# Graph layer on one core: group 3's gathers one stage later, the next-to-last batch in front of the last pieces, part of the last batch's products ahead of its sums

## The chip, the cores and the metric

The kernel runs on one core of a Trainium2 chip. The metric is the device time of one execution in microseconds. Its engines are TensorE (PE, with its weight loads as PEld), VectorE (DVE), ScalarE (ACT), GpSimd (POOL) and SyncE (SP); each works through its own instructions in program order and waits on semaphores for the others. Sixteen DMA engines move the data. "Group", "batch" and "stage" are explained below. Line numbers such as L618 are those of the kernel before.

## The reference, cut to what matters

One message-passing layer on a graph of 6250 nodes (128 features) and 100000 edges (4 features each), with the edges sorted by destination, and a layer norm on either side of the residual:

```python
msg_in = concatenate([x[src], x[dst], edge_attr], axis=1)
h = silu(msg_in @ mW1 + mb1)
messages = h @ mW2 + mb2
aggregated = segment_sum(messages, dst, num_segments=N)
u = silu(concatenate([x, aggregated], axis=1) @ uW1 + ub1)
updated = u @ uW2 + ub2
y = layer_norm(x + updated, ln_g, ln_b)
out = _layernorm(x + y)
```

All numbers are float32.

## The kernel before

**Set-up stage (L115 to L412).** The product of `msg_in` and `mW1` is split. Two tables are made from x: `tab_a` = x times the rows of `mW1` for the source, `tab_b` = x times the rows for the destination, plus `mb1`. The 49 tiles of 128 nodes are taken in seven parts of eight tiles (`parts`, L354), one part a turn of the loop at L367. In a turn TensorE first turns the next part's tiles around (`turn_x`, L336 to L341; ScalarE copies the result to `xT`), then makes the two tables of this part (L377); ScalarE copies one half (L379), VectorE adds the bias to the other (L380), and SP stores both to DRAM (L383, L384). The last product of each turn is kept in the list `table`. All TensorE results of this stage go through one ring of four PSUM buffers (`wide`).

**Gathers.** The rows of the edges' sources are gathered by GpSimd with indirect DMAs of 128 rows each (`fetch`, L273 to L294, gathers at L277), eight for a group of 1024 edges. There are 98 groups; the last has six tiles. The first five groups (0 to 4, `RAW` = 5) gather rows of x itself, since the table isn't ready, and TensorE multiplies them later (`turn_rows`, L357; L621); the others gather rows of `tab_a`. `fetch(g, *after)` can take two instructions of TensorE: the first of the group's eight gathers then waits for the first of them, the fifth for the second; `None` is no wait. In the set-up stage the gathers are issued at these places: groups 0 and 1 ahead of the loop; `fetch(2, *table)` in turn 1 (waits for the products of turns 0 and 1); `fetch(3, None, table[2])` in turn 2 (the fifth gather waits for the products of turn 2); `fetch(4, *table[3:])` in turn 4 (products of turns 3 and 4); `fetch(RAW, None, turn_rows(2))` after the loop (group 5, which reads `tab_a` and waits for its stores).

**The loop over groups (L675 to L717).** For group g: SP loads rows of `tab_b` and edge attributes for group g+4 (`load`, L580); VectorE adds the gathered rows to TensorE's products (L635) and ScalarE takes the Silu (L636), both in `hidden`; TensorE makes the products of group g+2 (`products`, L618); VectorE makes the 0/1 matrices (`node_matrix` L591, `edge_matrix` L604); TensorE sums the messages by node with 0/1 matrices (`sums`, L647, 16 instructions for eight tiles, after a transpose of the degrees at L642 in every fourth group); VectorE adds the sums to `acc` and, every fourth group, the degrees to `deg` (`add`, L660 and L665). The gathers of group g+2 are issued in turn g; the first waits for the first product of group g+2, the fifth for the first sum of group g (L704).

**Batches of nodes (`node_batch`, L466 to L559).** When all edges of four tiles of nodes have been seen, a batch of these nodes is started, in stages divided by `yield`; the batch is a generator, and `advance` takes each running batch one stage further. The stages are: 1 load of x (L495, after a fill of the unused rows at L494 in the last batch) and, but for the last batch, copies of sums and degrees (L500, L501); 2 the products of x, sums and degrees (L509, L510, L511); 3 the Silu (L514); 4 the bias `ub2` as a product with a row of ones (L516) and the output product (L525); 5 addition of x and moments (L527, L483, L484; L530 adds `b_b` to x); 6 the root (L489); 7 the scaling, the addition of x and the moments of that (the "z stage", L534 to L540, L483, L484); 8 the root of these; 9 their reciprocal and the shift (L547, L549); 10 the output (L555); 11 the store (L559). The loop takes one stage a group, and two from group 92 on (L716). There are twelve batches in the list and a last one of two tiles. The twelfth, of three tiles, called `before` in the code and "the next-to-last batch" here, starts in group 95.

**The end (L719 to L756).** The last group, of six tiles, is done in two pieces of four and two tiles (`piece`, L726 to L729: addition L727, Silu L728, sums L647). The order around them is written out by hand: two more stages of the next-to-last batch, stage 1 of the last batch, the last full group's sums added, piece one, one stage of the next-to-last batch (its z stage), piece two, the last group's sums added, two stages of the last batch, then both batches in turn to their ends. The next-to-last batch has four stages behind it when the loop ends.

Of the kernel before, what the change touches and what calls it, by code (L numbers as in the profile page):

```python
# [18 lines left out]
P = 128  # L19
# [5 lines left out]
def kernel(  # L25
# [247 lines left out]
    def fetch(g, *after):  # L273

        rows[g] = gath.tile([P, G, H], F32, name="ga")
        for i in range(tiles_of(g)):
            ins = nc.gpsimd.indirect_dma_start(  # L277
                out=rows[g][:, i, :],
                out_offset=None,
                in_=x if g < RAW else tab_a[:, :],  # L280
                in_offset=bass.IndirectOffsetOnAxis(
                    ap=src_i[:, g, i : i + 1] if g else src_0[:, i : i + 1], axis=0
                ),
            )
            part, at = divmod(i * len(after), G)
            if after and at == 0 and after[part]:
                tc.add_manual_dep(
                    ins.ins,
                    after[part].ins.name,
                    mybir.DependencyInfo(  # L290
                        mybir.DependencyClass.Sync, mybir.DependencyReason.DATA
                    ),
                    reason="TensorE keeps up with the gathers",
                )  # L294
# [72 lines left out]
    for k, (i0, n) in enumerate(parts):  # L367
        if k + 1 < len(parts):
            turn_x(*parts[k + 1])

        tb = x_sb[:, i0 : i0 + n, :]
        ta = tpool.tile([P, G, H], F32, name="t", bufs=2)
        for j0, m in groups(n, G // 2):
            pm = wide().rearrange("p (i s) f -> p i s f", s=2)
            for j in range(m):
                cols = slice((i0 + j0 + j) * P, (i0 + j0 + j + 1) * P)
                ins = nc.tensor.matmul(pm[:, j], xT[:, cols], w1, start=True, stop=True)  # L377
            own = slice(j0, j0 + m)
            nc.scalar.copy(ta[:, own], pm[:, :m, 0, :])  # L379
            nc.vector.tensor_add(  # L380
                tb[:, own], pm[:, :m, 1, :], b1[:, None, :].to_broadcast([P, m, H])
            )
        nc.sync.dma_start(by_node(tab_a)[:, i0 : i0 + n, :], ta[:, :n])  # L383
        nc.sync.dma_start(by_node(tab_b)[:, i0 : i0 + n, :], tb)  # L384
        table.append(ins)
        if k == 0:
            attributes(0)
        if k == 1:
            fetch(2, *table)
            for t in mv:  # L390
                nc.sync.dma_start(t[W:], mW1[2 * H :])
        if k == 2:
            fetch(3, None, table[2])
        if k == 3:
            destination_lists()
            attribute_rows(0)
            turn_rows(0)
        cols = slice(i0 * P, NW if i0 + n == NT else (i0 + n) * P)
        nc.vector.memset(acc[:, cols], 0.0)
        if k == 4:  # L400
            fetch(4, *table[3:])
            destinations(0)
            load_bases(0)
            turn_rows(1)
# [27 lines left out]
    ub2_row = consts.tile([1, H], F32, name="ub2_row")  # L432
    g_b = consts.tile([P, H], F32, name="g_b")
    b_b = consts.tile([P, H], F32, name="b_b")
    raw_w = {}

    def load_weights():
        for name, shape in (("w2", [P, H]), ("u1a", [P, H]), ("mb2", [P, 1])):
            raw_w[name] = work.tile(shape, F32, name=f"raw_{name}", bufs=1)
        nc.sync.dma_start(raw_w["w2"], mW2)  # L440
        nc.sync.dma_start(raw_w["u1a"], uW1[P:])
        nc.sync.dma_start(raw_w["mb2"], mb2.rearrange("(f o) -> f o", o=1))
        nc.sync.dma_start(u1x, uW1[:P])
        nc.sync.dma_start(u2, uW2)
        nc.sync.dma_start(ub1_col, ub1.rearrange("(f o) -> f o", o=1))
        nc.sync.dma_start(ub2_row, ub2.rearrange("(o f) -> o f", o=1))
        for t, row in ((g_b, ln_g), (b_b, ln_b)):
            nc.sync.dma_start(t, row.rearrange("(o f) -> o f", o=1).to_broadcast([P, H]))

    def fuse_weights():  # L450
# [15 lines left out]
    def node_batch(i0, n, work, new, y, final=False):  # L466

        cols = slice(i0 * P, (i0 + n) * P)
        m = (min((i0 + n) * P, N) - i0 * P) // n
        assert m * n == min((i0 + n) * P, N) - i0 * P  # L470

        def rows_of(t):

            return t[i0 * P : i0 * P + m * n].rearrange("(p j) f -> p j f", j=n)

        def flat(t):
            return t[:, :n].rearrange("p i f -> p (i f)")

        def moments(v):
            mv = work.tile([P, BT, 2], F32, name="mv", bufs=2)  # L480
            for i in range(n):
                st = work.tile([P, 6], F32, name="st", bufs=2)
                nc.vector.bn_stats(st, v[:, i, :])  # L483
                nc.vector.bn_aggr(mv[:, i, :], st)  # L484
            return mv

        def std(mv):
            r = work.tile([P, BT], F32, name="r", bufs=2)
            nc.scalar.activation(r[:, :n], mv[:, :n, 1], AF.Sqrt, bias=eps)  # L489
            return r  # L490

        xs = new("xs")
        if m < P:
            nc.vector.memset(xs[m // 32 * 32 :, :n], 0.0)  # L494
        nc.sync.dma_start(xs[:m, :n], rows_of(x))  # L495
        sums, counts = acc[:, cols], deg[:, cols]
        if not final:

            acc_b, deg_b = new("acc_b"), new("deg_b", DR)
            nc.scalar.copy(flat(acc_b), sums)  # L500
            nc.scalar.copy(flat(deg_b), counts)  # L501
            sums, counts = flat(acc_b), flat(deg_b)
        yield
        xb = xs
        if final:
            xb = new("xb")
            nc.vector.tensor_add(xb[:, :n], xs[:, :n], b_b[:, None, :].to_broadcast([P, n, H]))
        y = y()
        nc.tensor.matmul(flat(y), u1x, xT[:, cols], start=True, stop=False)  # L509
        nc.tensor.matmul(flat(y), w2u, sums, start=False, stop=False)  # L510
        nc.tensor.matmul(flat(y), mb2u, counts, start=False, stop=True)  # L511
        yield
        uT = new("uT")
        nc.scalar.activation(flat(uT), flat(y), AF.Silu, bias=ub1_col)  # L514
        yield
        nc.tensor.matmul(  # L516
            y[:, :n],
            ones[0:1, :],
            ub2_row[:, None, :].to_broadcast([1, n, H]),
            start=True,  # L520
            stop=False,
        )
        by_p = flat(uT).rearrange("k (p j) -> k p j", j=n)
        for i in range(n):
            nc.tensor.matmul(y[:, i, :], by_p[:, :, i], u2, start=False, stop=i == n - 1)  # L525
        yield
        nc.vector.tensor_add(y[:, :n], y[:, :n], xs[:, :n])  # L527
        mv = moments(y)
        if not final:
            nc.vector.tensor_add(xs[:, :n], xs[:, :n], b_b[:, None, :].to_broadcast([P, n, H]))  # L530
        yield
        r = std(mv)
        yield
        nc.vector.reciprocal(r[:, :n], r[:, :n])  # L534
        z = new("z")
        for i in range(n):
            nc.vector.scalar_tensor_tensor(
                y[:, i, :], y[:, i, :], mv[:, i, 0:1], g_b, op0=OP.subtract, op1=OP.mult
            )
            nc.vector.scalar_tensor_tensor(  # L540
                z[:, i, :], y[:, i, :], r[:, i : i + 1], xb[:, i, :], op0=OP.mult, op1=OP.add
            )
        mz = moments(z)
        yield
        rz = std(mz)
        yield
        nc.vector.reciprocal(rz[:, :n], rz[:, :n])  # L547
        shift = work.tile([P, BT], F32, name="shift", bufs=2)
        nc.vector.scalar_tensor_tensor(  # L549
            shift[:, :n], mz[:, :n, 0], -1.0, rz[:, :n], op0=OP.mult, op1=OP.mult  # L550
        )
        yield
        o = z
        for i in range(n):
            nc.scalar.activation(  # L555
                o[:, i, :], z[:, i, :], AF.Identity, bias=shift[:, i : i + 1], scale=rz[:, i : i + 1]
            )
        yield
        (nc.scalar if final else nc.sync).dma_start(rows_of(out), o[:m, :n])  # L559
# [115 lines left out]
    for g in range(NG):  # L675
# [37 lines left out]
        for i0, n, first in batches[:-1]:  # L713
            if g == (first if first >= NG - 3 else first + 1):
                running.append(node_batch(i0, n, *node_tiles(nodes, node_y)))
        for _ in range(2 if g >= NG - 6 else 1):  # L716
            advance(running)  # L717

    g = NG - 1  # L719
# [18 lines left out]
    )  # L738
    while running:
        advance(running)  # L740
    for _ in range(2):
        next(before)
    next(final)

    nc.scalar.activation(primed, ones[0:1, 0:1], AF.Silu)
    add(g - 1, pt.pop(g - 1))
    pt[g] = degrees(g)
    piece(0, n - 2)
    next(before)
    piece(n - 2, n)  # L750
    add(g, pt.pop(g))
    for _ in range(2):
# [161 lines left out]
```

## Time and profile before

| | us |
|---|---|
| median of 3 runs | 1183.07 (1181.99 to 1183.82) |
| the profiled execution | 1183.82 |
| its span, first to last instruction | 1181.7 |
| TensorE busy | 738.3 |
| GpSimd busy | 743.1 |
| VectorE busy | 486.0 |
| ScalarE busy | 239.8 |

The mean clock granted to TensorE is 0.667 of full speed. A line of the timeline has the start and duration in us, the engine, the line of the kernel, the operation, what it writes and reads ("out<-in"), and in brackets the idle time of its engine just before it with what ended it; "remote" is a semaphore whose sender the profile doesn't identify, "issue" is time in which it shows no wait. A line of the groups has the number of instructions, the total and mean duration, and the idle time before them. TensorE's instructions are recorded at their start, and their ends are modelled. A product of float32 shows as two instructions.

### The profile page before, as it was taken

To read this page: it belongs to the slowest core of one execution; us is meant where nothing else is said; L and a number is where in the kernel's file an instruction comes from. 1 tells how busy PE (TensorE), PEld (TensorE's weight loads), DVE (VectorE), ACT (ScalarE), POOL (GpSimd) and SP (SyncE) were. 2 spreads that over 40 slices of the span, in tenths; PEclk is the share of its full clock that TensorE was granted. 3 is DMA by queue.
4 is the path that set the end of the run, shared out by engine and by line. 5 is a ranking of instruction groups with operands and counts; after the bars stand their busy time and mean duration, and the time that the engine had idled before them with its cause. 6 is when DMAs were issued, how large, how long until landed. Compare 5 with 4: busy or idle time off the path is not lost.

```text
span 1181.7 us, 11311 instructions
## 1 busy us (share of the span) xinstructions
PE 738.3 (62%) x3647; PEld 668.7 (57%) x3647; DVE 486.0 (41%) x1016; ACT 239.8 (20%) x297; POOL 743.1 (63%) x790
## 2 busy tenths in 40 slices
PE   5466887655765566557646655756666665656653
PEld 4465775645655565556645654656565565656552
DVE  4361653432523532532443353343343252353344
ACT  2110120320311221220221121121132131122132
POOL 6546666666666566656666665666566666666660
PEclk9787877666566567566666666666666667666665
DMA  8662232232222231223132222232222222222120
GB/s 200 181 167 73 73 82 64 67 82 64 70 67 73 56 81 50 77 65 84 47 83 71 59 57 80 67 81 56 70 74 66 72 72 62 65 56 69 46 59 20
DMA packets 69932, 88.95 MB, mean 75 GB/s; under 512 B 20687, under 2 KB 51550, under 8 KB 69866
## 3 DMA queue, kind: packets, MB, share of 16 engines
q0 software_dynamic: 25024, 51.30, 17.1%
q1 hardware_dynamic: 40264, 34.96, 10.2%
q10 hardware_dynamic: 4578, 1.89, 0.7%
q8 instruction: 31, 0.51, 0.2%
q14 instruction: 35, 0.29, 0.1%
HBM read 76.71 MB, written 11.38 MB: 75 GB/s over the span
## 4 chain that ended last, share of the span: by engine, by line
PE 44%; issue 35%; POOL 12%; DMA 3%; DVE 2%; another core or an unknown queue 2%; SPq 1%; ACT 1%; DVEq 0%; ACTq 0%; POOLq 0%
PE pre L618 20%; PE pt L647 16%; POOL ga L277 12%; PE y L525 2%; PE wide L377 1%; DMA ga<-tab_a,src_i 1%; PE y L516 1%; PE y L509 1%; PE pre L621 1%; PE y L510 1%; PE wide L339 1%; DVE s L635 1%; DMA x_sb<-in_x_dram 1%; PE y L511 1%
## 5 line engine op out<-in xcount | busy, mean ns | idle before, releaser
L277 POOL DMA_INDIRECT ga<-tab_a,src_i x742 | 703.7, 948 | 383.1 <-issue 200.4
L618 PE MATMUL pre<-mv,st 100*128 100x128 f32 x1564 | 343.3, 393 | 227.3 <-issue 197.6
L618 PEld LDWEIGHTS pre<-mv,st 100*128 100x128 f32 x1564 | 314.2, 300 | 244.5 <-issue 219.3
L647 PE MATMUL pt<-oh,h 128*128 128x96 f32 x1564 | 290.6, 345 | 158.2 <-issue 149.3
L647 PEld LDWEIGHTS pt<-oh,h 128*128 128x128 f32 x1564 | 276.8, 262 | 179.4 <-issue 172.3
L635 DVE TENSOR_TENSOR s<-ga,pre 128x1024 f32<-128x1024 f32 x92 | 112.3, 1221 | 504.1 <-DMA ga<-tab_a,src_i 417.2
L636 ACT ACTIVATE h<-s 128x1024 f32<-128x1024 f32 x92 | 97.2, 1057 | 670.1 <-issue 379.8
L591 DVE TENSOR_SCALAR_CACHE_REDUCE st<-near,p_next 96x1024 f32<-96x1024 uint8 x98 | 124.2, 1268 | 4.2 <-DMA near<-near_d 1.5
L604 DVE TENSOR_TENSOR oh<-w_row,rel 128x768 f32<-128x768 f32 x98 | 93.0, 949 | 39.1 <-remote 36.4
L277 POOL DMA_INDIRECT ga<-in_x_dram,src_i x32 | 30.5, 954 | 21.7 <-issue 8.8
L527 DVE TENSOR_TENSOR y<-y,xs 128x512 f32<-128x512 f32 (+1 forms) x12 | 8.3, 688 | 80.8 <-issue 75.2
L636 ACT ACT_TABLE_LOAD x23 | 29.5, 1283 | 26.4 <-DMA b_b<-in_L_gnn_ln_b_dram 19.5
L489 ACT ACT_TABLE_LOAD x24 | 30.8, 1283 | 6.1 <-DVE st L483 5.7
L525 PEld LDWEIGHTS y<-u,uT 128*128 128x128 f32 x94 | 22.7, 327 | 10.2 <-issue 10.2
L514 ACT ACTIVATE uT<-y,ub_col 128x512 f32<-128x512 f32 (+1 forms) x12 | 8.2, 680 | 98.7 <-remote 58.8
L660 DVE TENSOR_TENSOR acc<-acc,pt 128x96 f32 x98 | 23.6, 241 | 8.9 <-PE pt L647 4.5
L525 PE MATMUL y<-u,uT 128*128 128x128 f32 x94 | 25.2, 416 | 0.0
L665 DVE TENSOR_TENSOR deg<-deg,pt 1x96 f32 x98 | 24.4, 249 | 1.0
L377 PE MATMUL wide<-w,xT 128*128 128x256 f32 x98 | 23.3, 391 | 1.1 <-issue 1.1
L621 PE MATMUL pre<-w,ga 128*128 128x128 f32 x80 | 18.9, 315 | 3.6 <-issue 3.4
L377 PEld LDWEIGHTS wide<-w,xT 128*128 128x128 f32 x98 | 18.8, 198 | 3.9 <-issue 1.5
L555 ACT ACTIVATE z<-z,shift,r 128x128 f32<-128x128 f32 x47 | 19.4, 482 | 0.4 <-DVE shift L549 0.4
(119 smaller groups left out, 357.3 us busy)
## 6 DMA issues: line engine op xcount, KB each, us to landing
ga<-tab_a,src_i POOLq DMA_INDIRECT x742
near<-near_d SPq DMA_DIRECT2D x24, 384.0 KB
mv<-tab_b SPq DMA_DIRECT2D x98, 48.0 KB
tab_a<-t SPq DMA_DIRECT2D x6, 512.0 KB
tab_b<-x_sb SPq DMA_DIRECT2D x6, 512.0 KB
xs<-in_x_dram SPq DMA_DIRECT2D x11, 256.0 KB
out_dram<-z SPq DMA_DIRECT2D x11, 256.0 KB
st<-ea_d SPq DMA_DIRECT2D x98, 16.0 KB
```

The costliest lines, as they stand in the source:

```text
L277: ins = nc.gpsimd.indirect_dma_start(out=rows[g][:, i, :], out_offset=None, in_=x if g < RAW else tab_a[:, :], in_offset=bass.IndirectOffs ...
L377: ins = nc.tensor.matmul(pm[:, j], xT[:, cols], w1, start=True, stop=True)
L489: nc.scalar.activation(r[:, :n], mv[:, :n, 1], AF.Sqrt, bias=eps)
L525: nc.tensor.matmul(y[:, i, :], by_p[:, :, i], u2, start=False, stop=i == n - 1)
L591: nc.vector.tensor_scalar(stbuf[g % NST][:W], near.pop(g), p_next, 0.0, op0=OP.is_equal, op1=OP.add, accum_out=deg_q[g // DQ % 2][:, g % D ...
L604: nc.vector.tensor_tensor(oh, w_row[:, None, :].to_broadcast([P, G, W]), rel[:, g, :, None].to_broadcast([P, G, W]), op=OP.is_equal,)
L618: ins = nc.tensor.matmul(pre[:, i, :], st[:, i, :], mv[g % NM], start=True, stop=g >= RAW)
L621: ins = nc.tensor.matmul(pre[:, i, :], rows[g][:, i, :], w1[:, 0, :], start=False, stop=True)
L635: nc.vector.tensor_add(s[:, :n], ga[:, :n], ps[:, :n])
L636: nc.scalar.activation(h[:, :n], s[:, :n], AF.Silu)
L647: ins = nc.tensor.matmul(pt[:, :W], h[:, i, :], oh[:, i, :], start=i == 0, stop=i == tiles_of(g) - 1)
L665: nc.vector.tensor_add(at, at, pt[row, W:])
```

## The change

In the set-up stage the gathers of group 3 are issued in turn 3 instead of turn 2, with waits for the products of turns 2 and 3 (first and fifth gather) instead of none and turn 2.

A broadcast tile of `ub2` (`ub2_b`) is loaded with the other weights in group 1.

In every batch the product of the degrees (`mb2u`) comes before that of the sums (`w2u`). In the last batch the two products of x and degrees become a stage of their own, and the product of sums the next; its bias `ub2` is added to x on VectorE in stage 2, and the product with the row of ones is left out there, so that each tile's output product starts its own accumulation.

From group 95 on (groups 95 and 96, the last two that advance batches) four stages are taken a group instead of two, so the next-to-last batch has eight stages behind it when the loop ends. The stages written out at the end change with it: none of the next-to-last batch stands in front of or between the pieces, and the last batch's new stage 2 (products of x and degrees, the additions on VectorE) stands between the last full group's addition and piece one.

```diff
--- before.py
+++ after.py
@@ -389,9 +389,8 @@
             fetch(2, *table)
             for t in mv:
                 nc.sync.dma_start(t[W:], mW1[2 * H :])
-        if k == 2:
-            fetch(3, None, table[2])
         if k == 3:
+            fetch(3, *table[2:])
             destination_lists()
             attribute_rows(0)
             turn_rows(0)
@@ -432,6 +431,7 @@
     ub2_row = consts.tile([1, H], F32, name="ub2_row")
     g_b = consts.tile([P, H], F32, name="g_b")
     b_b = consts.tile([P, H], F32, name="b_b")
+    ub2_b = consts.tile([P, H], F32, name="ub2_b")
     raw_w = {}
 
     def load_weights():
@@ -444,7 +444,7 @@
         nc.sync.dma_start(u2, uW2)
         nc.sync.dma_start(ub1_col, ub1.rearrange("(f o) -> f o", o=1))
         nc.sync.dma_start(ub2_row, ub2.rearrange("(o f) -> o f", o=1))
-        for t, row in ((g_b, ln_g), (b_b, ln_b)):
+        for t, row in ((g_b, ln_g), (b_b, ln_b), (ub2_b, ub2)):
             nc.sync.dma_start(t, row.rearrange("(o f) -> o f", o=1).to_broadcast([P, H]))
 
     def fuse_weights():
@@ -505,24 +505,29 @@
         if final:
             xb = new("xb")
             nc.vector.tensor_add(xb[:, :n], xs[:, :n], b_b[:, None, :].to_broadcast([P, n, H]))
+            nc.vector.tensor_add(xs[:, :n], xs[:, :n], ub2_b[:, None, :].to_broadcast([P, n, H]))
         y = y()
         nc.tensor.matmul(flat(y), u1x, xT[:, cols], start=True, stop=False)
-        nc.tensor.matmul(flat(y), w2u, sums, start=False, stop=False)
-        nc.tensor.matmul(flat(y), mb2u, counts, start=False, stop=True)
+        nc.tensor.matmul(flat(y), mb2u, counts, start=False, stop=False)
+        if final:
+
+            yield
+        nc.tensor.matmul(flat(y), w2u, sums, start=False, stop=True)
         yield
         uT = new("uT")
         nc.scalar.activation(flat(uT), flat(y), AF.Silu, bias=ub1_col)
         yield
-        nc.tensor.matmul(
-            y[:, :n],
-            ones[0:1, :],
-            ub2_row[:, None, :].to_broadcast([1, n, H]),
-            start=True,
-            stop=False,
-        )
+        if not final:
+            nc.tensor.matmul(
+                y[:, :n],
+                ones[0:1, :],
+                ub2_row[:, None, :].to_broadcast([1, n, H]),
+                start=True,
+                stop=False,
+            )
         by_p = flat(uT).rearrange("k (p j) -> k p j", j=n)
         for i in range(n):
-            nc.tensor.matmul(y[:, i, :], by_p[:, :, i], u2, start=False, stop=i == n - 1)
+            nc.tensor.matmul(y[:, i, :], by_p[:, :, i], u2, start=final, stop=final or i == n - 1)
         yield
         nc.vector.tensor_add(y[:, :n], y[:, :n], xs[:, :n])
         mv = moments(y)
@@ -713,7 +718,7 @@
         for i0, n, first in batches[:-1]:
             if g == (first if first >= NG - 3 else first + 1):
                 running.append(node_batch(i0, n, *node_tiles(nodes, node_y)))
-        for _ in range(2 if g >= NG - 6 else 1):
+        for _ in range(4 if g >= NG - 3 else 2 if g >= NG - 6 else 1):
             advance(running)
 
     g = NG - 1
@@ -738,15 +743,13 @@
     )
     while running:
         advance(running)
-    for _ in range(2):
-        next(before)
     next(final)
 
     nc.scalar.activation(primed, ones[0:1, 0:1], AF.Silu)
     add(g - 1, pt.pop(g - 1))
     pt[g] = degrees(g)
+    next(final)
     piece(0, n - 2)
-    next(before)
     piece(n - 2, n)
     add(g, pt.pop(g))
     for _ in range(2):
```

## The prediction

> **What bounds the kernel now.** I read the page's chain and costliest groups, the waits of GpSimd, the timeline of 0 to 130 us and of the last 100 us, and the stage table by ten microseconds.
>
> ```profile
> PE 44%; issue 35%; POOL 12%; DMA 3%; DVE 2%; another core or an unknown queue 2%; SPq 1%; ACT 1%; DVEq 0%; ACTq 0%; POOLq 0%
> L277 POOL DMA_INDIRECT ga<-tab_a,src_i x742 | 703.7, 948 | 383.1 <-issue 200.4
> ```
>
> Neither engine is full. A gather holds GpSimd for 0.95 us and the next begins 1.25 us after it. From 200 us on the waits of GpSimd repeat every 23.2 us: 16 gathers (20.0 us), then one wait of about 3.4 us for TensorE. One such wait, from the timeline:
>
> ```profile
> 1104.86 0.94 POOL L277 DMA_INDIRECT ga<-tab_a,src_i  x1 [0.30 <-issue]
> 1107.52 0.32 PE L647 MATMUL pt<-oh,h 128*128 128x96 f32 x1 [1.08 <-issue]
> 1108.92 2.24 PE L647 MATMUL pt<-oh,h 128*128 128x96 f32 x10 [1.08 <-issue]
> 1109.03 0.69 ACT L514 ACTIVATE uT<-y,ub_col 128x512 f32<-128x512 f32 x1 [9.19 <-remote]
> 1109.30 0.94 POOL L277 DMA_INDIRECT ga<-tab_a,src_i  x1 [3.50 <-remote]
> ```
>
> Late in a run of gathers TensorE takes one product per 1.4 us, and what it finished is seen late: the Silu at 1109.03 needs products recorded at 1092.6 to 1095.4. Some 3 us after the last gather TensorE takes ten in one go and everybody is released. I read this as: **a long run of gathers holds TensorE back, and a pause of GpSimd lets it catch up.** The same happens in the set-up stage, where it costs most:
>
> ```profile
> 32.59 3.62 PE L377 MATMUL wide<-w,xT 128*128 128x256 f32 x16
> 34.95 0.59 ACT L379 COPY t<-wide 128x512 f32<-128x512 f32 x1 [2.98 <-PE wide L377]
> 36.21 0.94 POOL L277 DMA_INDIRECT ga<-in_x_dram,src_i  x1 [0.30 <-issue]
> ...
> 44.97 0.94 POOL L277 DMA_INDIRECT ga<-in_x_dram,src_i  x1 [0.30 <-issue]
> 46.92 1.01 ACT L340 COPY xT<-wide 128x1024 f32<-128x1024 f32 x1 [11.39 <-remote]
> 49.14 1.08 ACT L379 COPY t<-wide 128x512 f32<-128x512 f32 x2 [1.20 <-remote]
> 49.42 0.94 POOL L277 DMA_INDIRECT ga<-in_x_dram,src_i  x1 [3.51 <-remote]
> ```
>
> The gathers of 36.21 to 44.97 are group 3's. From 37.3 to 46.9 no other engine works: the transposes that ScalarE copies at 46.92 were recorded before 33 us. TensorE's results come out 1.0 us (46.92) to 3.5 us (49.42) after the last gather ended at 45.91. The first run does the same: gathers end at 23.11, ScalarE goes on at 23.80, GpSimd at 26.21.
>
> The tail:
>
> ```profile
> 1149.86 0.26 DVE L660 TENSOR_TENSOR acc<-acc,pt 128x96 f32 x1 [4.28 <-remote]
> 1149.92 0.58 ACT L514 ACTIVATE uT<-y,ub_col 128x384 f32<-128x384 f32 x1 [4.03 <-remote]
> 1153.93 1.65 PE L525 MATMUL y<-u,uT 128*128 128x128 f32 x6
> 1155.67 0.57 DVE L527 TENSOR_TENSOR y<-y,xs 128x384 f32<-128x384 f32 x1 [5.56 <-PE y L525]
> 1159.13 0.69 DVE L727 TENSOR_TENSOR s<-ga,pre 128x512 f32<-128x512 f32 x1
> 1163.22 0.40 DVE L727 TENSOR_TENSOR s<-ga,pre 128x256 f32<-128x256 f32 x1
> 1165.32 0.26 DVE L660 TENSOR_TENSOR acc<-acc,pt 128x96 f32 x1 [1.71 <-PE pt L647]
> 1167.94 0.48 ACT L514 ACTIVATE ga<-pre,ub_col 128x256 f32<-128x256 f32 x1 [3.87 <-PE pre L511]
> 1168.47 1.22 PE L516 MATMUL pre<-ub_row,ones 1*128 1x256 f32 x2 [0.57 <-ACT ga L514]
> ```
>
> It is one serial chain: the next-to-last batch's products (to 1155.6), VectorE's work on them, the pieces of the last group, the last batch. Only its links can be shortened.
>
> **What the Trainium skill says.** "TensorE: Matmul & The Clock Gate", What's actually happening: the clock halves after an idle window of about 3.4 us. The trace fits: the last set-up product is taken at 36.2 and the clock falls near 39.2. So the half clock follows from the stall and doesn't cause it. "Advanced Engine Details and Errata", Engine Queue Depths: TensorE queues 64 instructions[...]. "ScalarE: Activation LUTs", What ACT_TABLE_LOAD costs: 1283 ns; the trace has 1283. On what gathers do to TensorE I found nothing there that I use; that rests on this trace.
>
> **The change, part by part.**
>
> (1) Group 3's gathers are issued one stage later on GpSimd, the second four waiting for the products of stage 3. The first four still start at 36.21 (group 2's end at 35.9, stage 2 is done by 34.95), and end at 40.9. Now GpSimd pauses there instead of at 45.91. If the pause frees TensorE, what came 3.5 us after 45.91 comes 3.5 us after 40.9: stage 3's products at 44.4 and not 49.42, and ScalarE and VectorE follow 5.0 us earlier. Queued behind the new wait: the rest of group 3, then group 4. Eight gathers now run from 44.4 to 54.1 where four ran. The second run of before fell behind after about 6 us, at about 32 (the transposes recorded from 31.7). If this one does too, at 50, the products of stage 4 (recorded 56.7 to 60.4 before, so 51.7 to 55.4 now) come only in the pause after 54.1, at up to 54.1+3.5 = 57.6, and GpSimd goes on there and not at 60.63: a gain of 3.0. A backlog of 40 products instead of 24 makes it about 1 less. So −5.0 to −2.0; I take **−3.4** for the start. It passes through if group 5's gathers, which wait at 73.47 for the last table store, move as much; the store follows the same TensorE stages.
>
> (2) One more broadcast load on SP after 82.68: 0.43 us by its neighbours. SP's next issue that waits is at 85.03, behind 83.16+0.43, so 1.4 us of cover; without it, 0.4. I take 0.
>
> (3) Counts before sums in every batch: the same six products; the copy of the counts ends at 1139.45, where the first product starts. 0.
>
> (4) Four stages a group in the last two groups. The Silu of the next-to-last batch now stands before the last full group's Silu on ScalarE, and its eight bias and output products before that group's sums on TensorE. The Silu was released at 1149.92, with two other engines (1149.86, 1149.88), 2.5 us after GpSimd paused; nothing before that point gets shorter, so I keep 1149.92. Queued behind it: the group's Silu, which ran at 1144.83 and now runs at 1150.50 to 1151.56. Products: 1150.5 + 1.57 + 1.6 = 1153.7 (before 1155.6). Then transpose and 16 sums: 0.3 + 16×0.22 = 3.8, to 1157.6, which nobody needs before 1159.9.
> VectorE from 1153.8: add and moments 1.9, ScalarE's root 0.35 and the rest of L530, then the z stage without the piece, 3.5 (L534 at 1159.73 to 1163.22): 1159.6. Next-to-last batch done, but all of it in front of the pieces.
>
> (5) The last batch's x load is issued after its 0.27 us fill, at 1159.95. Before: issue 1158.42, bytes done by 1160.25, so some 2.0 us: 1162.0. The two additions (0.42 each) now stand before the pieces and wait for it: piece one 1162.9 (before 1159.13), piece two 1163.5 (before 1163.22). Price of the wait: 1.3 us, after 0.8 of degrees work in its cover. ScalarE and TensorE: first sums 1.47 after the piece, 1164.3, twelve in 3.0; the last add at 1167.3 (before 1165.32): **+2.0**.
>
> (6) After it only the product of sums remains: add to Silu 1.4 instead of 2.62: **−1.2**. The bias products go: **−1.2** (1.22). ScalarE must fit three L555 (1.27) and a table load (1.28) into the 2.7 us to the root; it does. The added VectorE addition is in (5).
>
> Tail: 2.0−1.2−1.2 = **−0.4**. Ends: if the Silu's products were seen when recorded (1144.4), part (4) would start up to 5 us sooner; group 97's last gathers, issued to 1152.1, and TensorE then limit the gain to about 3.5. On the other side a slower x load or sums give +1.
>
> Sum: −3.4−0.4 = −3.8. The profiled execution took 1183.82 (span 1181.7, 2.1 around it): 1180.0. The median is 0.75 below that one: **1179.3**.
>
> **Rivals.**
> A, the pause doesn't free TensorE; the stall ends by itself near 46. For: the stretch may be TensorE's own limit after 20 us at full load. Against: it ends after the last gather each time I looked, and the tail without gathers shows none. Start 0, tail −0.4: 1182.7.
> B, slower: as A, and the moved gathers collide. Stage 3 still at 49.42, then eight gathers to 59.1 instead of four; stage 4's products wait for the pause: 59.1+3.5 = 62.6 and up to 1 more, against 60.63, +2 to +3; with a tail of 0 to +1: 1186. It decides when stage 3 is seen after about 47.4, since eight gathers from there end at 57.1 and 3.5 more is 60.6.
> C, the tail's Silu is released early: −3.5 and −3.4: 1176.2.
>
> **Chances.** Forecast 0.47 (own range 1175.5 to 1181.5; 0.07 of it within 0.2%), A 0.22, B 0.19, C 0.12. 0.2%, about what can be told from no change here, is 2.4 us. Faster 0.40+0.12 = 0.52, same 0.07+0.22 = 0.29, slower 0.19. Range 1175.5 to 1186: it leaves out about half of B and a little of C.
>
> **What would show it.** Right: a pause of GpSimd near 41, stage 3's copies near 44, group 5's first gather near 70; the next-to-last Silu near 1150 less the start's gain and before the group's Silu; pieces back to back after the x load; no bias product at the end. Wrong: ScalarE's copy still at 46.9 after a pause at 41 (A), group 4's second half after 60.6 (B), or a changed rhythm of waits between 100 and 200 us, which would shift the total by its own amount.

## The result, and the profile after

The changed kernel takes **1179.25 us** (median of 6 runs, 1175.96 to 1179.78) where the kernel before takes 1183.62 (6 runs beside it, 1181.99 to 1185.12): ratio **0.9958**, 95% interval 0.9944 to 0.9972. (The ratios here are worked out from all runs of both sides, so they differ a little from the quotient of the two medians.) The profiled execution took 1179.78, with a span of 1177.7, 4.0 below that of before. Line numbers in this section are those of the changed kernel; in the experiments, those of the kernel whose lines are shown.

The page after: the chain, and the costliest group.

```profile
PE 35%; issue 32%; POOL 20%; DVE 2%; DMA 1%; another core or an unknown queue 1%; ACT 1%; DVEq 0%; POOLq 0%; SPq 0%; ACTq 0%
L277 POOL DMA_INDIRECT ga<-tab_a,src_i x742 | 703.7, 948 | 384.2 <-issue 187.1
```

The gathers are the same 742 with the same 703.7 us, and their idle time has not changed either (384.2 against 383.1). The steady state is untouched. The gain lies at the start. The timeline after, from the second run of gathers on:

```profile
37.55 0.59 ACT L379 COPY t<-wide 128x512 f32<-128x512 f32 x1 [2.24 <-PE wide L377]
37.79 0.95 POOL L277 DMA_INDIRECT ga<-in_x_dram,src_i  x1 [2.00 <-remote]
38.04 1.02 ACT L340 COPY xT<-wide 128x1024 f32<-128x1024 f32 x1
38.94 1.09 ACT L379 COPY t<-wide 128x512 f32<-128x512 f32 x2
...
51.47 1.01 ACT L340 COPY xT<-wide 128x1024 f32<-128x1024 f32 x1 [10.47 <-remote]
55.39 0.94 POOL L277 DMA_INDIRECT ga<-in_x_dram,src_i  x1 [2.44 <-PE wide L339]
...
69.88 0.94 POOL L277 DMA_INDIRECT ga<-tab_a,src_i  x1 [9.79 <-DMA tab_a<-t]
```

GpSimd pauses for 2.00 us, and ScalarE's copy of the transposes (L340), at 46.92 before, comes at 38.04; the two copies of stage 3 come at 38.94 instead of 49.14. Twelve gathers in a row follow (37.79 to 52.95), and late in them TensorE is held once more: the next copy of transposes waits until 51.47, 1.5 us before the run ends. Group 4's second half goes on at 55.39 (60.63 before), and group 5, which waits for the last store of `tab_a`, at 69.88 (73.47). But the pause stands ahead of group 3's *first* gather and not, as predicted, ahead of its fifth: stage 2's second copy, seen at 34.95 before, came only at 37.55 in this execution. Of the 5.2 us that group 4's second half gained, 1.6 are lost again by group 5. The last 18 instructions of TensorE for the tables show where, at least in part, first before, then after:

```profile
61.17 4.05 PE L377 MATMUL wide<-w,xT 128*128 128x256 f32 x18
56.47 6.98 PE L377 MATMUL wide<-w,xT 128*128 128x256 f32 x18 [1.75 <-DVE x_sb L380]
```

The granted clock was 1.0 in the first stretch and 0.5 in the second until 62.2. In the repetition of the changed kernel (below) they take 4.05 us again, at a clock of 1.0, and group 5's wait is 8.15 us as before.

The tail of the changed kernel:

```profile
1145.80 0.26 DVE L665 TENSOR_TENSOR acc<-acc,pt 128x96 f32 x1 [4.80 <-remote]
1145.87 0.58 ACT L518 ACTIVATE uT<-y,ub_col 128x384 f32<-128x384 f32 x1 [7.50 <-remote]
1146.35 1.04 ACT L641 ACTIVATE h<-s 128x1024 f32<-128x1024 f32 x1
...
1149.82 0.57 DVE L532 TENSOR_TENSOR y<-y,xs 128x384 f32<-128x384 f32 x1 [3.76 <-PE y L530]
...
1158.25 0.43 DVE L507 TENSOR_TENSOR ga<-ga,b_b 128x256 f32<-128x256 f32 x1 [1.50 <-DMA ga<-in_x_dram]
...
1159.17 1.02 DVE L732 TENSOR_TENSOR s<-ga,pre 128x512 f32<-128x512 f32 x2
...
1163.49 0.26 DVE L665 TENSOR_TENSOR acc<-acc,pt 128x96 f32 x1 [3.30 <-PE pt L652]
...
1165.06 0.47 ACT L518 ACTIVATE ga<-pre,ub_col 128x256 f32<-128x256 f32 x1 [4.23 <-PE pre L515]
...
1172.79 0.60 ACTq L564 DMA_DIRECT2D out_dram<-ga  x1
```

The next-to-last batch's Silu is released at 1145.87, 4.05 earlier than before (1149.92): all that is gained by then. From it to the issue of the last store it is 26.92 us, and was 26.83 (1149.92 to 1176.75). So in this pair of traces the whole rebuilt tail is worth **+0.1 us**.

### The profile page after: what moved, and what is told of

Its sections match the earlier page's. It is cut to its first block, busy times and chain, and to the rows that moved or that the text cites. A ratio compares the mean times of both kernels' runs of the same rounds, so it can differ in the third digit from the quotient of the medians.

```text
span 1177.7 us, 11313 instructions
## 1 busy us (share of the span) xinstructions
PE 747.7 (63%) x3645; PEld 675.3 (57%) x3645; DVE 486.4 (41%) x1017; ACT 238.9 (20%) x297; POOL 743.2 (63%) x790
## 4 chain that ended last, share of the span: by engine, by line
PE 35%; issue 32%; POOL 20%; DVE 2%; DMA 1%; another core or an unknown queue 1%; ACT 1%; DVEq 0%; POOLq 0%; SPq 0%; ACTq 0%
POOL ga L277 20%; PE pre L623 17%; PE pt L652 14%; PE pre L626 1%; PE y L530 1%; DMA ga<-tab_a,src_i 1%; PE y L521 1%; PE y L510 1%; PE y L511 0%; PE y L515 0%; DVE s L640 0%; DVE st L483 0%; DVE oh L609 0%; PE pt L647 0%
## 5 line engine op out<-in xcount | busy, mean ns | idle before, releaser
L277 POOL DMA_INDIRECT ga<-tab_a,src_i x742 | 703.7, 948 | 384.2 <-issue 187.1
L652 PE MATMUL pt<-oh,h 128*128 128x96 f32 x1564 | 293.7, 348 | 147.6 <-issue 143.8
L652 PEld LDWEIGHTS pt<-oh,h 128*128 128x128 f32 x1564 | 279.9, 266 | 165.8 <-issue 162.3
L377 PE MATMUL wide<-w,xT 128*128 128x256 f32 x98 | 27.6, 441 | 3.5 <-DVE x_sb L380 3.5
L377 PEld LDWEIGHTS wide<-w,xT 128*128 128x128 f32 x98 | 21.5, 227 | 8.3 <-DVE x_sb L380 4.3
L521 PE MATMUL y<-ub_row,ones 1*128 1x512 f32 (+1 forms) x24 | 15.5, 729 | 6.9 <-ACT uT L518 6.9
```

What stands on the lines that cost most here:

```text
L277: ins = nc.gpsimd.indirect_dma_start(out=rows[g][:, i, :], out_offset=None, in_=x if g < RAW else tab_a[:, :], in_offset=bass.IndirectOffs ...
L521: nc.tensor.matmul(y[:, :n], ones[0:1, :], ub2_row[:, None, :].to_broadcast([1, n, H]), start=True, stop=False,)
L652: ins = nc.tensor.matmul(pt[:, :W], h[:, i, :], oh[:, i, :], start=i == 0, stop=i == tiles_of(g) - 1)
```

## The experiments

The theory: the pause of GpSimd inside group 3's gathers frees TensorE, and that is the whole gain; the tail gives and takes the same amount. The rivals: the gain sits in the tail; or group 3's gathers gain because they are later, or because of the first wait, and not because of a pause. The experiments ran on three other chips of the same kind, where the kernel before takes 1174.1 us (chip 7: start alone, tail alone, each wait alone), 1174.5 (chip 15: the pause without a wait, the early x load, the short links, the other order of the end) and 1175.2 (chip 12: the pause in the first run, the old order, the changed kernel again). So the ratios to the kernel before beside them are compared, and from the traces the lengths of stretches; the total times are set side by side only within one chip. The kernel before was traced on the first chip alone.

**Start alone, tail alone.** Only the moved `fetch(3)` in the kernel before:

```diff
-        if k == 2:
-            fetch(3, None, table[2])
         if k == 3:
+            fetch(3, *table[2:])
```

> The kernel before with group 3's gathers moved one stage later (both waits), nothing of the tail. My theory, that the set-up stage carries the whole gain (group 5's first gather came at 69.88 instead of 73.47, the last store's issue 3.96 us sooner): about 4 us below the kernel before, ratio 0.9965, group 5's first gather near 70. The rival, that the tail's new order gives half or more of it: 1 to 2 us below, ratio 0.9985 or more.

Measured 1169.39 us, ratio 0.9959 (0.9946 to 0.9972). And the reverse, the changed kernel with `fetch(3, None, table[2])` back in turn 2:

> The changed kernel with group 3's gathers put back where they were: all of the tail, nothing of the start. My theory: the tail's gains and losses cancel (+2.0, -1.2, -1.2 in the prediction; +0.1 by the two traces), so -0.5 to +0.5 us against the kernel before, ratio 1.000, group 5's first gather near 73.5. The rival, that the tail gives half or more: 2 us or more below.

Measured 1174.82, ratio 1.0011 (1.0003 to 1.0019). The start carries the gain and the tail loses a little: 0.9959 times 1.0011 is 0.9970. Group 5's first gather, with the start alone and with the tail alone:

```profile
68.89 0.95 POOL L277 DMA_INDIRECT ga<-tab_a,src_i  x1 [7.98 <-DMA tab_a<-t]
74.48 0.94 POOL L277 DMA_INDIRECT ga<-tab_a,src_i  x1 [8.11 <-DMA tab_a<-t]
```

On this chip the start moves it by 5.6 us, and not by the 3.6 of the first pair of traces. From the released Silu to the last store this kernel takes 26.72 us (1140.95 to 1167.67); so what it loses isn't in that stretch, and where it is stays open.

**Which wait.** The first gather's wait alone, at the old place:

```diff
-            fetch(3, None, table[2])
+            fetch(3, table[2], None)
```

> The kernel before, group 3 at its old place, but its first gather waits for the products of stage 2 and its fifth for nothing. In the changed kernel's trace GpSimd paused at this wait (35.79 to 37.79) and not at the fifth gather. If this wait is what frees TensorE: 3 to 4 us below the kernel before. If it is passed without a pause, as stage 2's result at 34.95 in the trace of before suggests, and the fifth gather's wait does the work, as predicted: within 1 us of the kernel before.

Measured 1174.06, ratio 0.9993 (0.9982 to 1.0003). And the fifth's alone, in turn 3:

```diff
-        if k == 2:
-            fetch(3, None, table[2])
         if k == 3:
+            fetch(3, None, table[3])
```

> The kernel before with group 3 one stage later, its first gather waiting for nothing and its fifth for the products of stage 3. This is the path that the prediction worked out: GpSimd stops near 41, stage 3's products come near 44.4, 2 to 5 us below the kernel before. If only the first gather's wait helps, as the changed kernel's trace reads: within 1 us of the kernel before, ScalarE's copy still near 46.9.

Measured 1169.96, ratio 0.9957 (0.9945 to 0.9969). First the timeline with the first wait alone, then that with the fifth alone:

```profile
48.98 1.07 ACT L379 COPY t<-wide 128x512 f32<-128x512 f32 x2 [3.28 <-remote]
49.26 0.94 POOL L277 DMA_INDIRECT ga<-in_x_dram,src_i  x1 [3.56 <-remote]
```

```profile
42.96 1.01 ACT L340 COPY xT<-wide 128x1024 f32<-128x1024 f32 x1 [6.47 <-remote]
43.38 0.94 POOL L277 DMA_INDIRECT ga<-in_x_dram,src_i  x1 [2.77 <-remote]
43.87 1.08 ACT L379 COPY t<-wide 128x512 f32<-128x512 f32 x2
...
56.15 0.94 POOL L277 DMA_INDIRECT ga<-in_x_dram,src_i  x1 [2.95 <-PE wide L361]
```

With the first wait alone nothing pauses until the eight gathers are through, as in the kernel before. Its single executions go down to 1169.58, so the wait may catch now and then, as it did in the changed kernel's profile; that was not traced. With the fifth alone GpSimd stands from 40.61 to 43.38, and stage 3's copies come at 43.87: the predicted course, about a microsecond sooner (44.4 was predicted for the end of the pause, and 57.6 at the latest for group 4's second half, which comes at 56.15).

**The pause without a wait.** Between group 3's fourth and fifth gather GpSimd fills a scratch tile three times, with the gathers at their old place and their old waits; nothing orders the fills by TensorE:

```diff
+            if pause and i == G // 2:
+                for _ in range(3):
+                    nc.gpsimd.memset(tpool.tile([P, GE], F32, name="idle"), 0.0)
...
-            fetch(3, None, table[2])
+            fetch(3, None, table[2], pause=True)
```

> The kernel before, with three fills of 128x1024 on GpSimd (into a tile that nothing reads) between the fourth and fifth gather of group 3: a pause of about 2.8 us by my estimate from 0.1 and 0.2 us for fills of 1 and 128 elements a partition, without any new wait for TensorE. If the pause itself is what lets TensorE catch up: ScalarE's copy near 43 instead of 46.9, as in the run with the fifth gather's wait alone, and 3 to 4.7 us below the kernel before. If it is the wait that orders things, and the pause does nothing: the copy still near 46.9 or later, 0 to 1 us slower than before.

Measured 1169.15, ratio 0.9957 (0.9943 to 0.9970). Its timeline, where the added lines shift the numbers by three:

```profile
39.59 0.94 POOL L280 DMA_INDIRECT ga<-in_x_dram,src_i  x1 [0.30 <-issue]
40.53 2.98 POOL L279 MEMSET idle<- 128x1024 f32 x3
42.91 1.01 ACT L343 COPY xT<-wide 128x1024 f32<-128x1024 f32 x1 [7.93 <-remote]
43.67 0.95 POOL L280 DMA_INDIRECT ga<-in_x_dram,src_i  x1 [0.16 <-issue]
```

Three microseconds of useless work on GpSimd make the kernel about 5 us faster. The copy at 42.91 comes 2.4 us after the last gather ended, while the fills still run: what frees TensorE is that no gather is being issued, not an idle GpSimd and not an order of waits. This is the run that rules out both rivals on the start.

**A pause in the first run too.** On top of the start alone, the second four gathers of group 1 wait for stage 0's products:

```diff
-    fetch(1)
     for k, (i0, n) in enumerate(parts):
...
         if k == 0:
+            fetch(1, None, table[0])
```

> The kernel before with group 3's gathers in turn 3 (the start alone), and the second four gathers of group 1 now wait for the products of turn 0, so that the first run of sixteen gathers is broken too. Theory (any pause of 2 to 3 us inside a run lets TensorE catch up, and the pause at the end of that run then shrinks): a pause near 18.4 to 20.5, the first copies of ScalarE from tables at about 20 instead of 23.80, a shorter wait than 3.09 us at 26.21, and group 2 no later than before by more than 1 us; all in all 0 to 2 us less than the start alone, ratio 0.9945 to 0.9959. Rival (each pause costs its length, and only the one in group 3's run pays): group 2 starts 2 to 3 us later, ratio 0.998 or more.

Measured 1171.25, ratio 0.9972 (0.9960 to 0.9983). The pause does what the theory says locally:

```profile
20.07 0.59 ACT L378 COPY t<-wide 128x512 f32<-128x512 f32 x1 [2.86 <-PE wide L376]
21.50 0.94 POOL L277 DMA_INDIRECT ga<-in_x_dram,src_i  x1 [3.42 <-PE wide L376]
26.50 0.95 POOL L277 DMA_INDIRECT ga<-in_x_dram,src_i  x1 [0.30 <-issue]
```

The first copy comes at 20.07 instead of 23.80, and the wait of 3.09 us that group 2 had is gone (0.30). But it buys nothing: one pause has taken the place of the other, and group 5's first gather begins at 69.05, while in the changed kernel on the same chip (below) it begins at 68.19. The likely reading is that a pause pays only where TensorE's backlog was holding up something on the path; no other run tests it. The total is neither what the theory nor what the rival had, and not told apart from the start alone.

**The x load's wait in the tail.** The changed kernel with the last batch created, and its x loaded, at the start of group 96:

```diff
+        if g == NG - 2:
+            final = last_batch()
+            next(final)
...
     while running:
         advance(running)
-    next(final)
```

> The changed kernel with the load of the last batch's x (and its fill) issued at the start of group 96 instead of after the next-to-last batch's z stage. In the changed kernel VectorE stood 1.50 us in front of L507 for this load. If that wait is on the path, as the prediction priced it: about 1.5 us below the changed kernel, so about 6 below the kernel before, ratio 0.995. If something else is late there: as the changed kernel, ratio 0.996.

Measured 1170.23, ratio 0.9962 (0.9948 to 0.9976): no difference from the changed kernel can be told. In the trace the wait ahead of L507 is gone and the stretch from the Silu to the last store is 24.98 us, 1.9 less than the changed kernel's. But the Silu itself was released late:

```profile
1138.77 0.58 ACT L518 ACTIVATE uT<-y,ub_col 128x384 f32<-128x384 f32 x1 [14.77 <-remote]
1139.25 1.05 ACT L650 ACTIVATE h<-s 128x1024 f32<-128x1024 f32 x1
```

The last full group's Silu (L650) stands behind the batch's and waits with it. But this order is not shown to make the release late. GpSimd makes its last fourteen gathers here in one run, without the pause ahead of the last two that the changed kernel's first trace has (to 1145.82). The Silu is released 2.85 us after the last of them ends. In every trace but that of the last experiment, with either order, it comes 2.5 to 3.3 us after a run of gathers ends: it looks like the hold of the set-up stage once more. Why the last pause falls now here and now there is open; the changed kernel has both courses in its two traces.

**That order by itself.** Two stages of the next-to-last batch in group 95 and six in group 96, and beside it the changed kernel once more:

```diff
-        for _ in range(4 if g >= NG - 3 else 2 if g >= NG - 6 else 1):
+        for _ in range(6 if g == NG - 2 else 2 if g >= NG - 6 else 1):
```

> The changed kernel, with the next-to-last batch taking two stages in group 95 and six in group 96 (instead of four and four): its Silu and its output product stand behind the Silu and the sums of the last full group, as they did before the change. Theory (the change's fourth part shortens the chain because the output product no longer stands behind sixteen sums): the addition that follows it comes 1.8 us later after the release than in the changed kernel (5.8 instead of 4.0), and the end with it; ratio to the kernel before 0.9973. Rival (the batch's Silu ahead of the group's Silu holds back ScalarE and TensorE as much as it gains): no difference or a gain, ratio 0.9958 or less, with the group's Silu some 5 us before the release.

> The changed kernel once more, unaltered, on the chip of the other experiments. If its gain doesn't depend on the chip: ratio to the kernel before 0.9958, give or take 0.0014. Theory (the fifth gather's wait is what counts, where the pause falls is a matter of a few tenths of a microsecond in the execution): the pause in the run of gathers may stand before the first or before the fifth gather of group 3, and group 5's first gather begins 3.5 to 5 us before that of the kernel before either way. Rival (the first gather's wait matters): a pause before the fifth gather would go with a smaller gain.

Measured: 1171.91, ratio 0.9975 (0.9968 to 0.9982), with the old order; 1170.67, ratio 0.9968 (0.9959 to 0.9976), for the changed kernel. The lines of the old order, then of the new one:

```profile
1131.28 1.06 ACT L641 ACTIVATE h<-s 128x1024 f32<-128x1024 f32 x1 [4.24 <-issue]
1136.49 0.58 ACT L518 ACTIVATE uT<-y,ub_col 128x384 f32<-128x384 f32 x1 [4.15 <-remote]
1142.51 0.57 DVE L532 TENSOR_TENSOR y<-y,xs 128x384 f32<-128x384 f32 x1 [5.77 <-PE y L530]
```

```profile
1138.79 0.58 ACT L518 ACTIVATE uT<-y,ub_col 128x384 f32<-128x384 f32 x1 [14.21 <-remote]
1139.27 1.05 ACT L641 ACTIVATE h<-s 128x1024 f32<-128x1024 f32 x1
1142.74 0.57 DVE L532 TENSOR_TENSOR y<-y,xs 128x384 f32<-128x384 f32 x1 [8.62 <-PE y L530]
```

From Silu to addition it is 6.02 us with the old order and 3.95 with the new one: the expected 1.8 to 2 us are there. But in these two executions the release came 2.3 us later with the new order, so the additions start 0.2 apart. That is not the order's doing either, as the run with the fifth wait alone shows, which has the old order throughout:

```profile
1138.29 0.58 ACT L513 ACTIVATE uT<-y,ub_col 128x384 f32<-128x384 f32 x1 [6.24 <-remote]
1142.24 0.57 DVE L526 TENSOR_TENSOR y<-y,xs 128x384 f32<-128x384 f32 x1 [5.10 <-PE y L524]
```

It too makes its last fourteen gathers without a pause. It has the late release (1136.06 with the start alone on the same chip) and, with it, the short link of 3.95. So in these traces the new order shortens the link only where GpSimd pauses before its last two gathers: to 3.95 in the changed kernel's first trace and with the tail alone, from 5.75 in the kernel before and 5.76 with the start alone. Both expectations are half right, and the totals don't separate them. In the repetition the pause stood ahead of group 3's fifth gather (from 40.65 to 43.38), as predicted, and not ahead of the first: the changed kernel does either.

**The short links alone.** The start, with part (6) only: the last batch's split products and `ub2` on VectorE, its two additions behind the last sum, and the pieces and the next-to-last batch in the old order. Against the changed kernel, the main lines:

```diff
         nc.tensor.matmul(flat(y), w2u, sums, start=False, stop=True)
         yield
+        if final:
+            xb = new("xb")
+            nc.vector.tensor_add(xb[:, :n], xs[:, :n], b_b[:, None, :].to_broadcast([P, n, H]))
+            nc.vector.tensor_add(xs[:, :n], xs[:, :n], ub2_b[:, None, :].to_broadcast([P, n, H]))
...
-        for _ in range(4 if g >= NG - 3 else 2 if g >= NG - 6 else 1):
+        for _ in range(2 if g >= NG - 6 else 1):
...
+    piece(0, n - 2)
     next(final)
-    piece(0, n - 2)
+    next(before)
     piece(n - 2, n)
```

> The start of the change, and of the tail only what shortens the last links: counts and x ahead of the sums, the bias on VectorE (its additions issued behind the last sums' add), with the pieces and the next-to-last batch in the order of before. The prediction's terms: -1.2 and -1.2. If they hold: 2.4 us below the start alone (ratio 0.996 there), so ratio 0.994. If the last batch's root then waits for ScalarE's other work (a table load of 1.28 and three outputs of 1.27 stand in front of it), only about -1.5: ratio 0.9945.

Measured 1167.92, ratio 0.9955 (0.9942 to 0.9968). From the Silu to the last store its trace has 24.37 us (1135.84 to 1160.21), against 26.83 with the start alone (1136.06 to 1162.89): −2.5, the size predicted for part (6). The totals differ by less than the intervals can tell.

**Another order of the end.** The start, the early x load, and the last pieces in front: the last full group's sums and piece one first, the next-to-last batch's products after it, its other stages in the gaps (cut):

```diff
-        for _ in range(4 if g >= NG - 3 else 2 if g >= NG - 6 else 1):
+        for _ in range(1 if g == NG - 2 else 2 if g >= NG - 6 else 1):
...
+    pt[g] = degrees(g)
+    piece(0, n - 2)
+    next(before)
+    add(g - 1, pt.pop(g - 1))
+    piece(n - 2, n)
+    next(final)
+    next(before)
+    add(g, pt.pop(g))
...
```

> A version meant to beat both: the start of the change, the early load of the last batch's x, and the end ordered by what is late: the last full group's Silu and sums first, then piece one, then the next-to-last batch's bias and output products, piece two as soon as its rows are there, and the rest of the next-to-last batch in the gaps of the last one. By my working from the trace of before, TensorE becomes the limit of the tail (sums, pieces and products without a gap from the release near 1150 to about 1163), and the last output is issued 6 to 7 us sooner than before; with the start 10 to 11 us below the kernel before, ratio 0.991. If the end isn't set by the order but by TensorE at half clock or by VectorE, 5 to 7 below: ratio 0.995.

Measured 1163.95, ratio **0.9919** (0.9904 to 0.9934), faster than both kernels, and 10.5 us below the kernel before by the medians, where 10 to 11 were expected:

```profile
1138.68 0.58 ACT L518 ACTIVATE uT<-y,ub_col 128x384 f32<-128x384 f32 x1 [7.04 <-PE pt L661]
1138.87 0.69 DVE L743 TENSOR_TENSOR s<-ga,pre 128x512 f32<-128x512 f32 x1
...
1147.88 0.25 DVE L674 TENSOR_TENSOR acc<-acc,pt 128x96 f32 x1
...
1149.16 0.47 ACT L518 ACTIVATE ga<-pre,ub_col 128x256 f32<-128x256 f32 x1
...
1157.72 0.60 ACTq L564 DMA_DIRECT2D out_dram<-ga  x1
```

Piece one starts 0.2 us after the release, where it starts 13.3 us after it in the changed kernel (1145.87 to 1159.17), and the last store is issued 19.04 us after the release instead of 26.92. (The batch's Silu stands behind the group's sums here, so its release is not quite the same point; counted from the start of the span the last store comes 2.5 us before that of the short links and 6.0 before that of the early x load on the same chip.) The next-to-last batch's work fills the gaps of VectorE and ScalarE in the last batch's chain.

## Why the prediction was right, point by point

| step | predicted | measured |
|---|---|---|
| (1) start, at group 5's first gather | −3.4 | −3.6 (73.47 to 69.88) |
| up to the Silu's release | 0 | −0.5 more (to −4.05) |
| (5) release to the last addition | +2.0 | +2.2 (15.40 to 17.62) |
| (6) addition to Silu | −1.2 | −1.05 (2.62 to 1.57) |
| (6) Silu to the last batch's first root | −1.2 | −1.08 (4.35 to 3.27) |
| tail, (4) to (6) | −0.4 | +0.1 |
| sum | −3.8 | −4.0 |

**The sum** is in part luck. Where start and tail ran apart, the start gave 4.7 us by the medians, where 3.4 were forecast, which lies at the edge of its interval (3.3 to 6.3); the tail cost 0.7 by the medians (0.4 to 2.2 by the interval), where it was to give 0.4. By these runs a start taken too small and a tail taken too kindly made up for each other.

**Step (1)** held in its mechanism, and this is shown: a pause frees TensorE whether a wait or plain work makes it. Its course in the changed kernel's trace was another. "Stage 2 is done by 34.95" failed there: the copy came at 37.55, so the first gather's wait caught and no pause was needed at 40.9. The repetition paused at the predicted place. The wait of the first gather alone doesn't bring the gain by its medians. That −3.6 lies so near −3.4 is luck too. The pause was taken as 3.5 us and was 2.0 to 2.8; stage 3 came 10.2 us earlier instead of 5.0, and group 4's second half 5.2 instead of 3.0; 1.6 of that went again, as group 5's wait for the table grew from 8.15 to 9.79 with the last products at half clock. The traces with the predicted course have neither the early stage 3 nor this loss: group 5's first gather moves by 5.4 us with the fifth wait alone (68.91, against 74.32 with the first alone on the same chip).

**Steps (2) and (3)** show nowhere: the idle time of the gathers is unchanged (384.2 against 383.1).

**Step (4)** kept the release where it was and found the link from Silu to addition 1.8 us shorter: 3.95 against 5.75. "1153.8" less the 4.05 gained gives 1149.75, and the trace has 1149.82. Putting the batch's Silu ahead of the group's ties the group to the release, which the prediction reckoned with; that this costs anything is not shown.

**Step (5)**: the price of the wait was 1.3 and is 1.50; the load took 2.17 us from issue to use, against 2.05 (1159.95 to 1162.0).

**Step (6)**'s two links are each 0.1 short of their size.

**Rivals.** A (the pause doesn't free TensorE) and B (the moved gathers collide) fall with the copies at 38.04 and with group 4 at 55.39, and again on the predicted path with 42.96 and 56.15 (fifth wait alone). C (an early release of the tail's Silu) did not occur: it came with GpSimd's pause.

## What to carry to other kernels

A long run of gathers can cost more in what it holds up than in its own length: look for results that are recorded but consumed only after the run, and break the run where they are due, with a wait or with other work of that engine. A second pause bought nothing here, so ask first whether the freed results lie on the path. In this tail it paid to put the longest remaining chain (the last group's pieces) first and let the other batch's work fill its gaps; regrouped the other way round, the tail gave back what its shorter links had gained. And a forecast that comes true in its sum can be off in its terms: run the parts apart.

## What was not expected of the hardware

Late in a run of gathers, which GpSimd issues every 1.25 us, TensorE's results come late: transposes recorded before 33 us were copied at 46.92. In all thirteen traces stage 3's two copies come 2.5 to 3.9 us after the last gather before the pause, whether that gather ends at 35.7, 40.6 or 45.9. It is no strict lock. Early in a run results come at once: in the changed kernel products recorded from 42.07 to 43.61 (modelled end) were read by VectorE at 43.65, six microseconds into a run. Single copies come before a run has ended, at 51.47 there (1.5 us before) and at 44.69 with the first wait alone (1.0 before).

Fills of 1.0 us each (128x1024, 2.98 for three) don't hold TensorE back, so it is not GpSimd's being busy. Nor is it the amount of data that the DMA engines move: from 42 to 46 us they moved 51 GB/s in the kernel before, where TensorE, VectorE and ScalarE stood, and 306 in the changed kernel, where VectorE read its results on time. Whether it is the making of the gathers' descriptors or something else that goes with them, and why TensorE's records run so far ahead of its results, no run here tells.
